# The causal mask of the second attention: a VectorE minimum instead of matmuls

## The chip, the cores and the metric

One core of one Trainium2 chip runs the whole program. The metric is the device time of one execution, in microseconds. The kernel before took 3099.48 us (median of 3 runs, 3081.88 to 3100.42).

## What is computed

Four stages over x of shape (4, 1024, 256), each with a residual sum and a layer norm: a gated linear attention, a mixture of experts, a differential attention, a second mixture of experts. The change lies in the third, whose core is:

```python
s1 = jnp.einsum('bhqd,bhkd->bhqk', q1, k1) * scale      # 16 heads, head dim 16, 1024 x 1024
s2 = jnp.einsum('bhqd,bhkd->bhqk', q2, k2) * scale
s1 = jnp.where(causal, neg, s1)
s2 = jnp.where(causal, neg, s2)
a1 = jax.nn.softmax(s1, axis=-1)
a2 = jax.nn.softmax(s2, axis=-1)
attn = a1 - lam[None, :, None, None] * a2
out = jnp.einsum('bhqk,bhkd->bhqd', attn, v)
```

There are 4 sequences x 16 heads x 2 maps = 128 causal maps of 1024 x 1024.

## The kernel before

`Layer1Attention` handles the maps four at a time. Four maps (two heads, two maps each) make one **pass**; there are 32 passes, four to a **unit** (half of one sequence's heads). Each map owns 32 of the 128 contraction rows of TensorE (head dim 16, one row more for a constant, the rest padding), so that the products of four maps can run at once in four row groups.

The softmax takes each row's maximum first. A pass therefore has two halves:

- `maxima` (L1303): for every query row, the maximum of the scores. Score products (L1323, tile `sc`, queries on partitions) fill one PSUM bank of 512 columns; VectorE reduces the bank's blocks of 128 keys to their maxima with the sign turned (L1330, into `top`). The lower triangle of 8 x 8 blocks is cut into nine banks (`banks`, L1293 to L1299): the first two hold the eight diagonal blocks, four each; the next four hold blocks 0 to 3 of one query row; the last three hold the rest. In blocks on the diagonal, keys after the query have to be kept out.
- `numerators` (L1358): the transposed scores (L1385, tile `sa`, keys on partitions), with the maximum subtracted by the extra contraction row, then the exponential on ScalarE (L1391) into `e`, and on GpSimd an affine select (L1401) that clears the part above the diagonal. `values_of` (L1427) multiplies `e` by the values into `oa`.

Between the halves, `least` (L1338) combines `top` on VectorE (L1344), transposes it on TensorE (L1348), copies it (L1350) and sends four rows into `qT` by DMAs on SP's queue (L1353). The second half of a pass runs 22 steps behind the first (`LAG`), so two passes overlap.

The order is written out by hand, in `steps`, and holds for TensorE, GpSimd, VectorE and ScalarE alike. A pass has `STEPS` = 20 steps. Step t takes bank t // 2 for maps 0 and 1 (t even) or maps 2 and 3 (t odd), for t up to 17, and beside it the numerators of an earlier pass for the other two maps. So each step has four streams of products: two `sc` and two `sa`, issued in turn, one product of each (zip_longest, and the `todo` loop). Each stream ends with its reduction or its exponential. A step with four blocks in its bank issues four products of 128 columns per map, one with a single row block issues one of 512. After every even step come the products of `values_of` for the item before; after any step at most one job: one that is due (the transposed output `tpo`, L1441; `least`; the output projection `yo` of an earlier sequence), or one that prepares the next unit (`inputs`, `turn` with `qkp`, `values` with `vp`, `to_slots` with `tps`). VectorE's and GpSimd's small work is put off and released by a budget per step (`put_off`, `catch_up`).

All `sc` and `sa` tiles share one pool of six PSUM banks (`pp`). A new tile takes the bank that was given back first in the order of the program. A step whose four streams have as many products each gives back in the order sc, sa, sc, sa; a step whose `sc` have more products than its `sa` gives back both `sa` first.

The mask before: in the diagonal banks, each map's first product is identity (bfloat16, 128 x 128) times a constant of 0 and -1e30 (L1316, 512 columns, all 128 rows), which opens the accumulation; the scores are then added to it. These two products per step (one for each map) are issued ahead of the step's other products, by the `next(halves[-1])` at the end of `maxima`. `set_up` makes the constants (L1119 to L1126), under the first expert layer. With nine banks in order, the diagonal ones are steps 0 to 3 of each pass: 4 steps x 2 products x 32 passes = 256.

Of the kernel before, what the change touches and what calls it, by code (L numbers as in the profile page):

```python
# [11 lines left out]

F32 = mybir.dt.float32
AF = mybir.ActivationFunctionType
ALU = mybir.AluOpType
# [3 lines left out]
P = 128  # L19
# [632 lines left out]
class Router:  # L652
# [58 lines left out]
    def work(self, plan, proj, norm):  # L711
# [89 lines left out]
        def choose(i, key):  # L801
# [7 lines left out]
            def begin():  # L809
                nonlocal steps  # L810
                steps = choice(c, sp, lg.t[:, 0:n, :], n, got)
                next(steps)

            j = add("DVE", 0.3, key, begin, [*cur["jc", i], done[0]], use=[lg])
            j = add("ACT", 0.3, key, lambda: next(steps), [j], table="exp")
            oh = [None]

            def pick():
                next(steps, None)
                oh[0] = sp.tile([P, n, E], F32, tag="oh", name="oh")  # L820
                nc.vector.tensor_tensor(oh[0], got[1], got[2], ALU.add)
# [229 lines left out]
class Layer1Attention:  # L1051
# [11 lines left out]
    QC = 512  # L1063
# [7 lines left out]
    def set_up(self, c, wqkT, bqk, wvT, bv, woT, bo, hnw, lqk, trig):  # L1071

        tc, nc, ident = c.tc, c.nc, c.ident
        UH, NS = self.UH, self.NS
        BIG = 3.0e38
        wp = self.wp

        wqk_s = wp.tile([P, DC, 2, 512], F32)
        nc.sync.dma_start(wqk_s, wqkT.rearrange("(c p) u f -> p c u f", p=P))
        wv_s = wp.tile([P, DC, D], F32)  # L1080
        nc.sync.dma_start(wv_s, wvT.rearrange("(c p) f -> p c f", p=P))
        wo_s = wp.tile([P, DC, D], F32)
# [12 lines left out]
        bo_b = wp.tile([P, D], F32)  # L1095
        nc.sync.dma_start(bo_b, bo.partition_broadcast(P))


        tr = wp.tile([P, NT, 2, 3, 8], F32)
        nc.sync.dma_start(tr, trig.rearrange("(t p) u k f -> p t u k f", p=P))  # L1100


        lam = wp.tile([P, AH, 2], F32)
        nc.vector.memset(lam, 1.0)
        ls = wp.tile([P, 2, AH], F32)
        with tc.tile_pool(name="a1_l", bufs=1, reuse_waits="tile") as lpool:
            lq = lpool.tile([P, 4, AH, HD], F32)
            nc.sync.dma_start(lq, lqk.partition_broadcast(P))
            lp = lpool.tile([P, 2, AH, HD], F32)
            nc.vector.tensor_tensor(lp[:, 0], lq[:, 0], lq[:, 1], ALU.mult)  # L1110
            nc.vector.tensor_tensor(lp[:, 1], lq[:, 2], lq[:, 3], ALU.mult)
            nc.vector.tensor_reduce(ls, lp, AX.X, ALU.add)
        nc.scalar.activation(ls, ls, AF.Exp)
        ld = wp.tile([P, AH], F32)
        nc.vector.tensor_tensor(ld, ls[:, 1, :], ls[:, 0, :], ALU.subtract)
        nc.vector.tensor_scalar(lam[:, :, 1], ld, LAMBDA_INIT, None, ALU.subtract)


        BF = mybir.dt.bfloat16  # L1119
        maskneg = wp.tile([P, 4, P], BF)  # L1120
        ident16 = wp.tile([P, P], BF)
        with tc.tile_pool(name="a1_k", bufs=1, reuse_waits="tile") as kp:
            mask32 = kp.tile([P, P], F32)
            make_causal_mask(nc, mask32, mask_val=-1e30)
            nc.vector.tensor_copy(maskneg, bc(mask32, 1, 4))
            nc.vector.tensor_copy(ident16, ident)  # L1126

        qks, vas, tops = [], [], []  # L1130
        for i in range(2):
            w = wp.tile([P, 2, NS, SL], F32, tag=f"qks{i}", name=f"qks{i}")
            nc.gpsimd.memset(w, 0.0)
            nc.gpsimd.memset(w[:, 1, :, HD : HD + 1], 1.0)
            qks.append(w)
        for i in range(2):
            va = wp.tile([P, NT, UH * VW + SL - VW], F32, tag=f"va{i}", name=f"va{i}")
            nc.gpsimd.memset(va, 1.0)
            vas.append(va)
            top = wp.tile([P, 4, NT, 8], F32, tag=f"top{i}", name=f"top{i}")  # L1140
            nc.gpsimd.memset(top, BIG)
            tops.append(top)
        self.wqk_s, self.wv_s, self.wo_s, self.bqk_b, self.bv_b, self.bo_b = wqk_s, wv_s, wo_s, bqk_b, bv_b, bo_b
        self.tr, self.lam, self.maskneg, self.ident16 = tr, lam, maskneg, ident16
        self.qks, self.vas, self.tops = qks, vas, tops

    def run(self, c, keep, B, combine):
# [20 lines left out]
    def steps(self, c, B, combine):  # L1168
        tc, nc, ident = c.tc, c.nc, c.ident
        UH, NG, NS, QC, NQ = self.UH, self.NG, self.NS, self.QC, self.NQ  # L1170
        pp, po, pm, bp, sp, ee, st = self.pp, self.po, self.pm, self.bp, self.sp, self.ee, self.st
        wqk_s, wv_s, wo_s, bqk_b, bv_b, bo_b = self.wqk_s, self.wv_s, self.wo_s, self.bqk_b, self.bv_b, self.bo_b
        tr, lam, maskneg, ident16 = self.tr, self.lam, self.maskneg, self.ident16
        xTs, o, kTs, qTs = {}, {}, {}, {}
        self.o = o

# [119 lines left out]
        banks = [([(i, i, i + 1) for i in range(4)], (slice(0, 4), slice(7, 8)), True)]  # L1296
# [6 lines left out]
        def maxima(n, t):  # L1303

            u, g = divmod(n, NG)
            kT, qT, top = kTs[u], qTs[u], self.tops[n % 2]
            k, pair = divmod(t, 2)
            parts, (ri, rk), diag = banks[k]
            halves = []
            for s in (2 * pair, 2 * pair + 1):  # L1310
                sl = slice(SL * s, SL * s + SL)

                def matmuls(s=s, sl=sl):
                    sc = pp.tile([P, QC], F32, tag="sc", name="sc")
                    if diag:
                        nc.tensor.matmul(  # L1316
                            sc, lhsT=ident16, rhs=maskneg.rearrange("p b k -> p (b k)"), start=True, stop=False,
                        )
                        yield
                    at = 0  # L1320
                    for m, (i, k0, k1) in enumerate(parts):
                        w = (k1 - k0) * P
                        nc.tensor.matmul(  # L1323
                            sc[:, at : at + w], lhsT=qT[sl, g, ts(i, P)], rhs=kT[sl, g, k0 * P : k1 * P],
                            start=not diag, stop=not diag or m == len(parts) - 1,
                        )
                        at += w
                        yield
                    out = top[:, s, ri, rk]
                    nc.vector.tensor_reduce(  # L1330
                        out, sc.rearrange("p (a b k) -> p a b k", a=out.shape[1], k=P), AX.X, ALU.max, negate=True,
                    )

                halves.append(matmuls())
                if diag:
                    next(halves[-1])
            return halves

        def least(n):
# [156 lines left out]
        for s in range(N * STEPS + LAG):  # L1496
            now = s
            catch_up(ROOM)
            n1, t1 = divmod(s, STEPS)
            n2, t2 = divmod(s - LAG, STEPS)  # L1500
            first = maxima(n1, t1) if n1 < N and t1 < STEPS - 2 else []
            second = numerators(n2, t2) if n2 >= 0 else []

# [13 lines left out]
            u, k = divmod(s, US)  # L1517
            if u + 1 < U and k == LAG + 2:
                prep = prepare(u + 1)
            if s % (2 * US) == LAG + 4 and s > 2 * US:  # L1520
                b = s // (2 * US) - 1
# [249 lines left out]
```

## Time and profile before

| | |
|---|---|
| median of 3 runs | 3099.48 us (3081.88 to 3100.42) |
| profiled execution, its own time | 3090.43 us |
| its span, first to last instruction | 3088.7 us |
| mean granted TensorE clock | 0.978 |
| stage of the second attention, from the first mask product to the last reduction | 1266.4 to 2762 us |
| 1152 reductions, L1330 | 738.8 us busy, 685 ns each |

The columns of the views used below. A busy row gives an engine's busy time, its share of the span, and the number of instructions. The chain of work that ended last is followed back from the last instruction; its shares tell which engine's and which line's work set the end. A row of a group or of the timeline has the line, engine, operation, output tile <- input tiles, partitions x elements and the count; in the groups the busy time and the mean of one in ns stand behind the bar, then the idle time of the engine before them with what ended it; in the timeline each row begins with start and length in us. A wait row reads: who waited, for whom, us in total, times, the longest. PE is TensorE's products and PEld its weight loads; the ends of products are modelled, since they are pipelined, so the distance from one start to the next tells more than a length.

### The profile page before, as it was taken

Reading aid. Unit: us, or ns where it says so; the run is one execution under the profiler, and the core shown is the slowest. Engines: PE = TensorE matmul, PEld = TensorE weight load, DVE = VectorE, ACT = ScalarE, POOL = GpSimd, SP = SyncE. Lnnn points to the kernel's source line nnn. Section 1 sums busy time; section 2 is a strip of 40 time slices with the busy share of each in tenths; the row PEclk is TensorE's granted clock in tenths of the full one; section 3 lists DMA queues with packets and bytes.
Section 4 is the critical chain, followed back from the end, with each engine's and each line's share of the span. In section 5 each row is a group of like instructions: output and inputs, shape, how many; then the busy total and the mean of one; then the engine's idle time right before and its main releaser. Section 6 shows DMA issues by size and latency. Waiting matters only on the chain.

```text
span 3088.7 us, 49688 instructions
## 1 busy us (share of the span) xinstructions
PE 2962.2 (96%) x19863; PEld 1803.9 (58%) x19880; DVE 1660.0 (54%) x3755; ACT 1127.7 (37%) x2175; POOL 1020.0 (33%) x1587
## 2 busy tenths in 40 slices
PE   9999999799999997899999999999999999999999
PEld 4656556588888886544554455454555555545544
DVE  4555566411111112776566775667666666652766
ACT  5444443111111111145554454544545455553000
POOL 1131333311111112174444644436444353231100
PEclk9999999899999998899999999999999999998999
DMA  9610101355554452000000000000000000001000
GB/s 336 206 42 14 42 18 65 126 188 184 187 176 174 179 187 100 5 25 5 2 1 7 18 7 2 1 3 22 7 2 2 2 1 2 2 2 57 18 18 19
DMA packets 83417, 189.32 MB, mean 61 GB/s; under 512 B 10145, under 2 KB 68274, under 8 KB 78194
## 3 DMA queue, kind: packets, MB, share of 16 engines
q0 software_dynamic: 15504, 119.03, 10.7%
q1 hardware_dynamic: 66322, 66.31, 6.7%
q8 instruction: 157, 2.57, 0.4%
q10 hardware_dynamic: 1360, 0.80, 0.1%
q14 instruction: 74, 0.61, 0.1%
HBM read 129.23 MB, written 56.36 MB: 60 GB/s over the span
## 4 chain that ended last, share of the span: by engine, by line
PE 85%; DVE 5%; POOL 4%; ACT 3%; issue 2%; DMA 1%; SPq 0%; POOLq 0%; DVEq 0%
PE sc L1323 16%; PE oa L1427 9%; PE sa L1385 9%; PE pj L141 9%; PE yp L141 7%; PE gpb L141 7%; PE upb L141 7%; PE ypb L141 7%; PE qkp L141 4%; PE tps L1227 2%; PE sc L1316 2%; POOL rows L854 2%; PE op L561 1%; DVE top L1330 1%; PE tpo L1441 1%
## 5 line engine op out<-in xcount | busy, mean ns | idle before, releaser
L1330 DVE TENSOR_REDUCE top<-sc 128x4 f32<-128x512 f32 x1152 | 738.8, 685 | 332.0 <-PE sa L1385 165.6
L1391 ACT ACTIVATE e<-sa 128x512 f32<-128x512 f32 (+1 forms) x1280 | 642.4, 553 | 716.8 <-PE sa L1385 487.6
L1385 PE MATMUL sa<-qT,kT 32*128 32x512 f32 (+3 forms) x3072 | 787.3, 526 | 0.7 <-DVE top L1330 0.4
L1323 PE MATMUL sc<-kT,qT 32*128 32x128 f32 (+2 forms) x5120 | 733.7, 384 | 4.2 <-DVE top L1330 4.2
L1323 PEld LDWEIGHTS sc<-kT,qT 32*128 32x128 f32 x5120 | 404.7, 189 | 279.7 <-DVE top L1330 125.5
L1401 POOL TENSOR_SCALAR_AFFINE_SELECT e<-e 128x256 f32<-128x256 f32 x512 | 202.0, 407 | 611.9 <-ACT e L1391 611.4
L1385 PEld LDWEIGHTS sa<-qT,kT 32*128 32x128 f32 x3072 | 310.3, 185 | 94.2 <-issue 35.2
L1020 DVE TENSOR_TENSOR hT<-upb,sgb 128x512 f32<-128x512 f32 x117 | 80.9, 692 | 504.5 <-PE upb L141 501.4
L1427 PE MATMUL oa<-e,va 128*32 128x512 f32 (+3 forms) x3072 | 318.7, 500 | 25.2 <-POOL e L1401 22.3
L141 PE MATMUL yp<-w,xT 128*128 128x512 f32 x512 | 229.8, 596 | 0.0
L141 PE MATMUL gpb<-nTb,w 128*128 128x256 f32 x936 | 222.9, 381 | 0.6 <-DVE nTb L1000 0.6
L141 PE MATMUL upb<-nTb,w 128*128 128x256 f32 x936 | 221.7, 380 | 0.0
L141 PE MATMUL ypb<-w,hT 128*128 128x256 f32 x936 | 208.5, 379 | 0.0
L141 PEld LDWEIGHTS gpb<-nTb,w 128*128 128x128 f32 x936 | 178.8, 191 | 25.5 <-DVE nTb L1000 1.0
L993 POOL DMA_INDIRECT xg<-rows,xi x78 | 73.7, 945 | 362.9 <-PE tx L997 350.0
L141 PEld LDWEIGHTS upb<-nTb,w 128*128 128x128 f32 x936 | 178.1, 190 | 24.3
L141 PEld LDWEIGHTS ypb<-w,hT 128*128 128x128 f32 x936 | 174.9, 190 | 22.2
L1019 ACT ACTIVATE sgb<-gpb 128x512 f32<-128x512 f32 x117 | 69.8, 597 | 282.5 <-PE gpb L141 282.5
L1427 PEld LDWEIGHTS oa<-e,va 128*32 128x32 f32 x3072 | 67.8, 109 | 178.3 <-issue 89.6
L141 PEld LDWEIGHTS yp<-w,xT 128*128 128x128 f32 x512 | 93.5, 190 | 98.6 <-issue 96.6
L1618 DVE SCALAR_TENSOR_TENSOR x<-yp,comb,x 128x256 f32<-128x256 f32 x256 | 121.9, 482 | 45.1 <-PE yp L141 38.7
L165 POOL TENSOR_TENSOR ln_r<-ln_v,neghalf 128x1 f32<-128x1 f32 x96 | 53.6, 559 | 252.3 <-DVE ln_v L162 252.0
(257 smaller groups left out, 3645.6 us busy)
## 6 DMA issues: line engine op xcount, KB each, us to landing
rows<-zeros SPq DMA_DIRECT2D x8, 4096.0 KB
f_outs<-yb SPq DMA_DIRECT2D x39, 256.0 KB
xTt<-in_xT SPq DMA_DIRECT2D x8, 512.0 KB
x<-in_x SPq DMA_DIRECT2D x32, 128.0 KB
out_x<-y SPq DMA_DIRECT2D x32, 128.0 KB
qT<-nmT SPq DMA_DIRECT2D x128, 4.0 KB
wi<-in_e_wiT SPq DMA_DIRECT2D x8, 256.0 KB
wo<-in_e_wo SPq DMA_DIRECT2D x8, 256.0 KB
```

Source lines behind the costliest of these rows:

```text
L141: nc.tensor.matmul(out, lhsT=l, rhs=r, start=i == 0, stop=i == len(pairs) - 1)
L854: s = nc.gpsimd.indirect_dma_start(self.rows, bass.IndirectOffsetOnAxis(ap=ri[0][:, k, t : t + 1], axis=0), xn[t].t, None)
L993: nc.gpsimd.indirect_dma_start(x, None, rows, bass.IndirectOffsetOnAxis(ap=xi[:, i, j : j + 1], axis=0))
L1019: nc.scalar.activation(sg, gps, AF.Silu)
L1020: nc.vector.tensor_tensor(hT[:, f : f + 2, :], ups, sg, ALU.mult)
L1323: nc.tensor.matmul(sc[:, at : at + w], lhsT=qT[sl, g, ts(i, P)], rhs=kT[sl, g, k0 * P : k1 * P], start=not diag, stop=not diag or m == len ...
L1330: nc.vector.tensor_reduce(out, sc.rearrange("p (a b k) -> p a b k", a=out.shape[1], k=P), AX.X, ALU.max, negate=True,)
L1385: nc.tensor.matmul(sc[:, at : at + QC - q0], lhsT=kT[sl, g, ts(j, P)], rhs=qT[sl, g, qc * QC + q0 : (qc + 1) * QC], start=True, stop=True,)
L1391: nc.scalar.activation(e[:, half, 0:w], sc[:, 0:w], AF.Exp)
L1401: nc.gpsimd.affine_select(out=e[:, :, at : at + P], in_=e[:, :, at : at + P], pattern=[[0, 2], [1, P]], compare_op=ALU.is_ge, fill=0.0, ba ...
L1427: nc.tensor.matmul(oa[SL * s : SL * s + SL, q0:QC], lhsT=va[:, j, h * VW : h * VW + SL], rhs=es_[n, k, s // 2][:, s % 2, at : at + QC - q0 ...
L1618: nc.vector.scalar_tensor_tensor(acc, yp[:, k, :], comb[:, t % NT, e : e + 1], acc, ALU.mult, ALU.add)
```

## The change

The mask products go, and with them both constants. `set_up` makes one constant `most` (128 x 128, float32): 3.0e38 on and below the diagonal, -1e30 above it. In a diagonal bank the score products now open their own accumulation; VectorE then takes the minimum of the bank and `most` (repeated four times) into an SBUF tile `sm`, and the reduction reads `sm` instead of the bank. The bank is given back by the minimum. The order of the nine banks differs between the map pairs: the two diagonal banks come at steps 2 and 10 for maps 0 and 1, at steps 7 and 15 for maps 2 and 3.

```diff
-        BF = mybir.dt.bfloat16
-        maskneg = wp.tile([P, 4, P], BF)
-        ident16 = wp.tile([P, P], BF)
-        with tc.tile_pool(name="a1_k", bufs=1, reuse_waits="tile") as kp:
-            mask32 = kp.tile([P, P], F32)
-            make_causal_mask(nc, mask32, mask_val=-1e30)
-            nc.vector.tensor_copy(maskneg, bc(mask32, 1, 4))
-            nc.vector.tensor_copy(ident16, ident)
+        most = wp.tile([P, P], F32)
+        nc.gpsimd.memset(most, BIG)
+        nc.gpsimd.affine_select(
+            out=most, in_=most, pattern=[[-1, P]], compare_op=ALU.is_ge, fill=-1e30, base=0, channel_multiplier=1,
+        )
...
-            parts, (ri, rk), diag = banks[k]
+            parts, (ri, rk), diag = banks[((2, 0, 3, 4, 5, 1, 6, 7, 8), (2, 3, 4, 0, 5, 6, 7, 1, 8))[pair][k]]
...
                     sc = pp.tile([P, QC], F32, tag="sc", name="sc")
-                    if diag:
-                        nc.tensor.matmul(
-                            sc, lhsT=ident16, rhs=maskneg.rearrange("p b k -> p (b k)"), start=True, stop=False,
-                        )
-                        yield
                     at = 0
-                    for m, (i, k0, k1) in enumerate(parts):
+                    for i, k0, k1 in parts:
                         w = (k1 - k0) * P
                         nc.tensor.matmul(
                             sc[:, at : at + w], lhsT=qT[sl, g, ts(i, P)], rhs=kT[sl, g, k0 * P : k1 * P],
-                            start=not diag, stop=not diag or m == len(parts) - 1,
+                            start=True, stop=True,
                         )
                         at += w
                         yield
+                    if diag:
+                        full, sc = sc, sp.tile([P, QC], F32, tag="sm", name="sm")
+                        nc.vector.tensor_tensor(
+                            sc.rearrange("p (b k) -> p b k", k=P), full.rearrange("p (b k) -> p b k", k=P),
+                            bc(most, 1, QC // P), ALU.min,
+                        )
                     out = top[:, s, ri, rk]
                     nc.vector.tensor_reduce(
                         out, sc.rearrange("p (a b k) -> p a b k", a=out.shape[1], k=P), AX.X, ALU.max, negate=True,
                     )

                 halves.append(matmuls())
-                if diag:
-                    next(halves[-1])
```

More of the change, by code (lines that the diff above doesn't have):

```diff
@@ L9 @@
 from concourse.bass import ts
-from concourse.masks import make_causal_mask, make_identity
+from concourse.masks import make_identity
 from concourse._compat import with_exitstack
@@ L1143, in set_up @@
         self.wqk_s, self.wv_s, self.wo_s, self.bqk_b, self.bv_b, self.bo_b = wqk_s, wv_s, wo_s, bqk_b, bv_b, bo_b
-        self.tr, self.lam, self.maskneg, self.ident16 = tr, lam, maskneg, ident16
+        self.tr, self.lam, self.most = tr, lam, most
         self.qks, self.vas, self.tops = qks, vas, tops
@@ L1172, in steps @@
         wqk_s, wv_s, wo_s, bqk_b, bv_b, bo_b = self.wqk_s, self.wv_s, self.wo_s, self.bqk_b, self.bv_b, self.bo_b
-        tr, lam, maskneg, ident16 = self.tr, self.lam, self.maskneg, self.ident16
+        tr, lam, most = self.tr, self.lam, self.most
         xTs, o, kTs, qTs = {}, {}, {}, {}
```

## The prediction

> **What bounds the kernel now.** I read the page first, for the place of the second attention in the span and in the chain of work that ended last; then the span cut into passes; then lines 1316, 1323 and 1330 and their waits; then single steps in the timeline.
>
> ```profile
> PE 2962.2 (96%) x19863; PEld 1803.9 (58%) x19880; DVE 1660.0 (54%) x3755; ACT 1127.7 (37%) x2175; POOL 1020.0 (33%) x1587
> ...
> PE sc L1323 16%; PE oa L1427 9%; PE sa L1385 9%; PE pj L141 9%; PE yp L141 7%; PE gpb L141 7%; PE upb L141 7%; PE ypb L141 7%; PE qkp L141 4%; PE tps L1227 2%; PE sc L1316 2%; POOL rows L854 2%; PE op L561 1%; DVE top L1330 1%; PE tpo L1441 1%
> ```
>
> On this page PE is the bound and the mask (L1316) is 2% of the chain, some 60 us. Three passes of the 32 (one pass is four attention maps, 20 steps), by the view of stretches; columns: stretch, length, busy time of PE, PEld, DVE, ACT, POOL, then clock and DMA:
>
> ```profile
> 1266.70:1292.50 25.80, 23.83 (x172) 16.91 (x171) 22.60 (x38) 1.59 (x2) 0.00 (x0) 0.74 0.00 1
> 1919.50:1972.50 53.00, 52.95 (x441) 27.19 (x442) 31.71 (x59) 26.84 (x55) 26.92 (x41) 1.00 0.01 2
> 2639.20:2681.10 41.90, 41.15 (x377) 20.71 (x377) 27.67 (x53) 21.39 (x45) 13.19 (x26) 1.00 0.01 2
> ```
>
> The first is pass 0, which has no numerators beside it. The second is pass 14, which also prepares the next unit (qkp, tps, vp). The third is pass 29, which prepares nothing. By the starts of L1323, 16 passes are like 29 (40.6 to 45.5 us), 14 like 14 (50 to 58 us), pass 31 has nothing behind it.
>
> PE reads busy nearly throughout, but the digits hide stalls inside a step. Two adjacent steps of pass 29:
>
> ```profile
> 2662.58 0.69 PE L1323 MATMUL sc<-kT,qT 32*128 32x512 f32 x1
> ...
> 2664.49 0.69 PE L1385 MATMUL sa<-qT,kT 32*128 32x512 f32 x1
> ...
> 2665.54 1.05 PE L1427 MATMUL oa<-e,va 128*32 128x512 f32 x5
> ```
> ```profile
> 2663.74 1.29 DVE L1330 TENSOR_REDUCE top<-sc 128x4 f32<-128x512 f32 x2 [0.24 <-PE sa L1385]
> ```
>
> A step that waits for nothing takes 1.07 us (1938.46 to the next group at 1939.53). These two take 2.96 instead of 2.14: the second half of the second step starts at 2664.49, just after the first reduction (2663.74 + 0.69 = 2664.43) and the first exponential have emptied a bank. Six banks serve four streams, so a step's last two banks are those the step before has to empty first. Over the stage:
>
> ```profile
> PEld sc L1323 <- DVE top L1330: 125.5, 185, 2.0
> ```
>
> And the price of the mask itself, in pass 14 (start, length):
>
> ```profile
> 1922.55 0.59 PE L1316 MATMUL sc<-maskneg,ident 128*128 128x512 bf16 x2
> 1923.07 0.37 PE L1323 MATMUL sc<-kT,qT 32*128 32x128 f32 x1
> ```
>
> Start to start, two mask products hold PE for 0.52 us; there are 128 such pairs, 67 us in all.
>
> Skill, first place. Pass 29 shows 41.15 of 41.90 us of PE and only 20.71 of PEld. The Trainium skill ("Trainium Kernel Development and Optimization", Performance Expectations) calls matmul busy time a bad measure, because matmuls are pipelined, and weight-load time a good one. Going by PE busy, the whole 67 us would come back; by the page, only passes like 14 are full and would return 14 x 4 x 0.52 = 29 us.
>
> **Part 1, mask products removed.** At most 128 x 0.52 = 67 us; at least nothing, where PE waits for a bank at the same place anyway.
>
> **Part 2, minimum added.** 256 of 128x512 f32, PSUM and SBUF in. Not in the trace; same operands and size as L1235:
>
> ```profile
> L1235 DVE TENSOR_TENSOR qk<-qkp,bqk_b 128x512 f32<-128x512 f32 x56 | 38.7, 691 | 70.9 <-PE qkp L141 70.9
> L1330 DVE TENSOR_REDUCE top<-sc 128x4 f32<-128x512 f32 x1152 | 738.8, 685 | 332.0 <-PE sa L1385 165.6 <-PE sc L1323 164.7 <-PE oa L1427 0.4
> ```
>
> I take 0.69. Bounds: 0.42 (L1449, 256 elements) and 0.80 (L1045, 256 elements, two inputs and a scalar). The reduction then reads SBUF: L1461 takes 0.275 for 128 elements and L1344 0.417 for 256, in line 0.70 for 512; I keep 0.69. Independent operations overlap (two reductions take 1.29), dependent ones don't: 0.03 from the end of L1443 to the start of L1445. A diagonal step's DVE block is therefore min 0.69, reduce to 1.41, min to 2.04, reduce to 2.74, counted from 0.03 after the products: 1.45 us more than the 1.29 of now, 186 us over 128 steps. Its two banks are free at 0.72 and 2.04.
>
> **Part 3, diagonal banks moved** from steps 0 to 3 of a pass to steps 2, 7, 10, 15. Queued behind the block on DVE are the next step's reductions: the first ends 3.4 us after the diagonal step's products (2.68 + 0.69), where now it ends 1.8 after them if the steps follow at once (1.07 + 0.03 + 0.69). PE issues in order, so a bank that comes late holds all four streams. The step after a diagonal one takes banks that ACT empties; the second one after it is the one that meets the late reduction.
>
> Walk through pass 29, from its start at 2639.20, with the durations above:
> - Steps 1 and 2. Now step 2 begins at 5.20, behind the products at 2.08 (yo), two mask pairs and step 1. Without masks it could begin at 4.02. But step 1's reductions are behind the DVE work of yo (L1558 to L162, 3.31 to 4.61) and the first ends at 5.3, so step 2 ends at 6.5 (now 6.37). Both masks between were cover for this wait.
> - Step 4 begins at 9.3 (now 9.20): of three mask pairs, 1.56 us, nothing is left.
> - Step 7 (diagonal) and 8: step 8 needs ACT's banks; ends at 19.0 (now 18.92). Step 9 needs the first reduction of step 8, at 20.6 behind the block: ends 21.7 instead of 20.56, 1.1 late.
> - Steps 10 and 15: the steps just behind them have two or four score parts and so hand on ACT's banks first; the steps two behind wait for ACT as now. The lag settles at 0.85.
> - End: +0.85, less the mask pair that opens the next pass, 0.52: **+0.33**.
>
> Same walk in pass 14: a job of 0.5 to 1.9 us stands behind most steps, so banks are free earlier than needed. Step 2 still waits for the yo chain (ends 6.5, now 6.87), step 4 ends 0.4 early, steps 7 to 12 keep and widen that to 0.7, since job and output separate step 9 from the block: -0.6 to -0.7, and -0.5 for the opening pair: **-1.1**.
>
> Pass 0 goes by DVE already, as its chain shows:
>
> ```profile
> 1271.65 1.14 PE sc L1323 x16
> 1272.79 18.02 DVE top L1330 x30
> ```
>
> Now 24.4 us to its last reduction (1266.39 to 1290.81). After: one step 1.09, 36 reductions at 0.60, 8 mins at 0.725: 28.5. **+4.1**, less one opening pair: +3.6.
>
> Sum: 14 x -1.1 = -15.4; 16 x 0.33 = +5.3; pass 0 +3.6; pass 31 +0.85: **-5.7 us**.
>
> **Edits with one answer.** Setup loses a cast (L1125, 0.42 us at 588.7) and a copy on DVE, keeps a memset and a select on POOL (0.23, 0.30); it lies under the first expert layer's products (PE 9 in those slices). Uncovered: under 1 us. No DMA is added or moved; SP still sends four rows per pass (L1353, 0.73 apart). But step 2 moves 1.2 us towards them: the last lands about 1.85 after its issue (2767.09 to 2768.9 in the tail), 4.5 after the pass starts, and the numerators of step 2 need it. Where yo stands in step 0 they wait longer for the reduction; in passes 1 to 9, without yo, this landing takes that place. POOL gets no step of its own; its selects follow ACT.
>
> **Rivals.**
> *Full gain.* PE is the bound and stalls merely move: -67 and pass 0's +4 give -63, 3030; half of it kept gives 3062. For it: 85% of the chain is PE. Against: 2662.58 to 2665.54 above.
> *DVE sets the pace (slower).* One mechanism: the reduction two steps behind a diagonal step, late at step 9 by 1.1 us, is late behind all four. Then each pass loses 4 x (1.1 - 0.52) = 2.3 us, 31 x 2.3 + 4 = +75; 3168. It decides from 1.3 us lost per diagonal step (+31 in all), 2.5 times the 0.5 that the walk gives; min and SBUF reduction each 0.15 longer would do it, since the block then reaches step 9 in passes like 14 too. For it: 125.5 us of waits now, DVE busy from 27.7 to 33.5 of 41.9. Against: steps 12 and 17 take banks from ACT.
> *No work saved.* If the score products were to start no earlier anywhere, only DVE's excess in pass 0 would show: +4, 3097, within the forecast's class.
>
> Skill, second place. PE waits 125.5 us for L1330 to empty banks. The Trainium skill ("TensorEngine Tiling (Array Packing)", PSUM Bottleneck) says that row tiling speeds up the products but not the emptying of PSUM, which can become the bottleneck; it speaks against this change. By the rule one would forecast the second rival, 3168; by the walk, the sum above.
>
> **How the numbers follow.** The profiled execution took 3090.43 us (span 3088.7, 1.7 around it); the median of three is 3099.48, their lowest 3081.88. The mean of these four is 3093; less 5.7: 3087. Chances: walk right within some 0.7 us per pass, 3066 to 3112, 0.55; full gain (3030 to 3066) 0.20; DVE pace (3112 to 3168) 0.25. For 8 in 10 I leave out the far half of each rival: 3045 to 3132. About 1% (31 us) is what a measurement can tell. Faster by more: the full gain and little else, 0.22; slower: most of the DVE case, 0.23; within: 0.55.
>
> **What would show it.** Right: PE busy falls by some 50 us without the span following; DVE rises by about 180; waits of L1323 for DVE rise from 125.5 to over 170; pass 0 about 29, pass 29 about 42, pass 14 about 52. Step 9 late in pass 29 and not in 14. Wrong: pass 29 at 40 (full gain) or 44 (DVE), mins far from 0.69, a wait for the landing of qT rows that outlasts the reduction.

## The result, and the profile after

The changed kernel takes 3121.3 us (median of 14 runs, 3107.33 to 3132.66), the kernel before 3096.9 us beside it (14 runs, 3081.88 to 3104.01). The ratio is 1.0086, 95% interval 1.0071 to 1.0101: slower by 24 us, where 6 us less was forecast. The profiled span is 3115.2 us against 3088.7, at a granted clock of 0.977 against 0.978.

The page of the kernel after, engines and chain:

```profile
PE 2959.6 (95%) x19624; PEld 1799.9 (58%) x19624; DVE 1818.6 (58%) x4009; ACT 1134.7 (36%) x2175; POOL 1018.4 (33%) x1587
...
PE sc L1317 11%; PE sa L1383 10%; PE pj L141 9%; PE oa L1425 8%; PE yp L141 7%; PE gpb L141 7%; PE upb L141 6%; PE ypb L141 6%; DVE top L1330 4%; PE qkp L141 4%; DVE sm L1325 2%; PE tps L1225 2%; ACT e L1389 2%; PE op L561 1%; POOL rows L854 1%
```

(Line numbers shift: the score products are now L1317, the minimum L1325, the reduction still L1330, the transposed scores L1383, their exponential L1389.) The mask is gone from the chain, and VectorE has taken its place and more: L1330 went from 1% to 4%, and the minimum has 2%. PE lost the 256 mask products, yet its busy time fell by only 2.6 us. The same three passes as before, in the view of stretches (length, busy PE, PEld, DVE, ACT, POOL, clock, DMA):

```profile
1265.67:1295.04 29.37, 25.76 (x162) 19.69 (x162) 27.52 (x45) 2.03 (x3) 0.00 (x0) 0.60 0.00 1
1933.87:1986.02 52.14, 51.53 (x432) 26.10 (x432) 36.01 (x67) 26.81 (x54) 26.43 (x40) 1.00 0.01 2
2666.79:2710.62 43.83, 41.94 (x368) 20.79 (x368) 32.88 (x61) 21.77 (x44) 13.13 (x26) 1.00 0.01 2
```

Pass 0 and pass 14 came as forecast (29 and 52); pass 29 did not: 43.83 us, where 42 was forecast and 44 had been named as the sign of VectorE setting the pace. It has nine PE records fewer than before and is 1.93 us longer.

The new instructions cost what was assumed (busy us and mean ns behind the bar, then the idle time of VectorE before them):

```profile
L1325 DVE TENSOR_TENSOR sm<-sc,most 128x512 f32<-128x512 f32 x256 | 175.4, 685 | 92.9 <-PE sc L1317 73.7 <-PE sa L1383 19.2
L1330 DVE TENSOR_REDUCE top<-sm 128x4 f32<-128x512 f32 x256 | 176.2, 688 | 8.8
L1330 DVE TENSOR_REDUCE top<-sc 128x4 f32<-128x512 f32 x896 | 569.7, 683 | 120.6 <-PE sa L1383 63.2 <-PE sc L1317 55.9
```

The minimum takes 0.685 us (forecast 0.69), and reading SBUF instead of PSUM saves the reduction nothing (688 against 683 ns). What changed is who waits. Waits of the weight loads for VectorE, over the stage:

```profile
PEld sc L1317 <- DVE top L1330: 92.9, 150, 3.3
...
PEld sa L1383 <- DVE top L1330: 65.3, 105, 1.4
...
PEld sc L1317 <- DVE sm L1325: 27.4, 45, 1.7
...
PEld sa L1383 <- DVE sm L1325: 6.4, 21, 1.0
```

They sum to 192 us. Before they were 136.7: the 125.5 us shown there, and 11.2 for the transposed scores. A reader who follows L1317 alone sees 120.3 us and calls it an improvement; the added waits stand in front of `sa`, the other user of the same six banks.

Where the 26.5 us of span came in, from the starts of each pass's first score product in both traces, after less before:

| | forecast | measured |
|---|---|---|
| 14 passes like pass 14 | -15.4 | -1.9 |
| 14 passes like pass 29 | +4.6 | +19.9 |
| passes 11 and 19 | +0.7 | +10.9 |
| pass 0 | +3.6 | +3.6 |
| pass 31 | +0.85 | +2.4 |
| ahead of the stage's first score product | 0 | -1.0 |
| after the stage's last score step begins | 0 | -7.3 |

The last row most likely belongs to the one execution of before: its granted clock was 0.84 in the 57 us around the last numerators, against 0.94 in the kernel after. Eleven other kernels below have 319.5 to 326.4 us there, and one 328.7; before had 329.3.

### The profile page after: what moved, and what is told of

The parts are those of the page before. It is cut to its first block, busy times and chain, and to the rows that moved or that the text cites. A ratio compares the mean times of both kernels' runs of the same rounds, so it can differ in the third digit from the quotient of the medians.

```text
span 3115.2 us, 49419 instructions
## 1 busy us (share of the span) xinstructions
PE 2959.6 (95%) x19624; PEld 1799.9 (58%) x19624; DVE 1818.6 (58%) x4009; ACT 1134.7 (36%) x2175; POOL 1018.4 (33%) x1587
## 4 chain that ended last, share of the span: by engine, by line
PE 80%; DVE 10%; ACT 3%; POOL 3%; issue 2%; DMA 1%; SPq 0%; POOLq 0%; DVEq 0%; another core or an unknown queue 0%
PE sc L1317 11%; PE sa L1383 10%; PE pj L141 9%; PE oa L1425 8%; PE yp L141 7%; PE gpb L141 7%; PE upb L141 6%; PE ypb L141 6%; DVE top L1330 4%; PE qkp L141 4%; DVE sm L1325 2%; PE tps L1225 2%; ACT e L1389 2%; PE op L561 1%; POOL rows L854 1%
## 5 line engine op out<-in xcount | busy, mean ns | idle before, releaser
L1389 ACT ACTIVATE e<-sa 128x512 f32<-128x512 f32 (+1 forms) x1280 | 646.5, 553 | 738.2 <-PE sa L1383 458.5
L1383 PE MATMUL sa<-qT,kT 32*128 32x512 f32 (+3 forms) x3072 | 830.6, 524 | 14.7 <-DVE top L1330 11.2
L1317 PE MATMUL sc<-kT,qT 32*128 32x128 f32 (+2 forms) x5120 | 732.3, 388 | 10.9 <-DVE top L1330 7.7
L1330 DVE TENSOR_REDUCE top<-sc 128x4 f32<-128x512 f32 x896 | 569.7, 683 | 120.6 <-PE sa L1383 63.2
L1317 PEld LDWEIGHTS sc<-kT,qT 32*128 32x128 f32 x5120 | 399.4, 189 | 236.2 <-DVE top L1330 92.9
L1383 PEld LDWEIGHTS sa<-qT,kT 32*128 32x128 f32 x3072 | 318.1, 184 | 151.6 <-DVE top L1330 65.3
L1325 DVE TENSOR_TENSOR sm<-sc,most 128x512 f32<-128x512 f32 x256 | 175.4, 685 | 92.9 <-PE sc L1317 73.7
L1330 DVE TENSOR_REDUCE top<-sm 128x4 f32<-128x512 f32 x256 | 176.2, 688 | 8.8
```

The lines of the kernel that those rows point to most:

```text
L1317: nc.tensor.matmul(sc[:, at : at + w], lhsT=qT[sl, g, ts(i, P)], rhs=kT[sl, g, k0 * P : k1 * P], start=True, stop=True,)
L1325: nc.vector.tensor_tensor(sc.rearrange("p (b k) -> p b k", k=P), full.rearrange("p (b k) -> p b k", k=P), bc(most, 1, QC // P), ALU.min,)
L1330: nc.vector.tensor_reduce(out, sc.rearrange("p (a b k) -> p a b k", a=out.shape[1], k=P), AX.X, ALU.max, negate=True,)
L1383: nc.tensor.matmul(sc[:, at : at + QC - q0], lhsT=kT[sl, g, ts(j, P)], rhs=qT[sl, g, qc * QC + q0 : (qc + 1) * QC], start=True, stop=True,)
L1389: nc.scalar.activation(e[:, half, 0:w], sc[:, 0:w], AF.Exp)
```

## The experiments

Each ratio is to the kernel before, run on the same chip between its runs, with its 95% interval.

### What is the removal worth, and what the order?

First, neither mask nor minimum. Here the maxima of the diagonal blocks take in keys after the query as well; the exponentials there are still cleared by GpSimd, and a quotient of exponentials doesn't depend on the number subtracted. `neither_new` is the kernel after with its order of banks, `neither_old` the same with the order of before.

```diff
# against the kernel after: neither_new
-                    if diag:
-                        full, sc = sc, sp.tile([P, QC], F32, tag="sm", name="sm")
-                        nc.vector.tensor_tensor(
...
# and for neither_old also
-            parts, (ri, rk), diag = banks[((2, 0, 3, 4, 5, 1, 6, 7, 8), (2, 3, 4, 0, 5, 6, 7, 1, 8))[pair][k]]
+            parts, (ri, rk), diag = banks[k]
```

> The old order of the banks, with neither mask products nor minimum: the maxima of the diagonal blocks then take in later keys too, which the select after the exponential still clears. Three theories for the 24 us lost. Queue (the mask's time does come back, and VectorE's block of minimum and reduction costs more than that through banks given back late): 3050 to 3065 us, passes like 29 about 1 us shorter than before, passes like 14 about 1.6 us. Cover (the mask products only filled waits for banks, their removal pays nothing): 3090 to 3100. Order (the new places of the diagonal banks are what costs): the full gain, 3030 to 3045.

> The kernel after without the minimum: new order, no mask of the maxima at all. Queue: 3050 to 3070, within 10 us of the same with the old order. Cover: 3090 to 3100. Order: 25 us or more above the same with the old order.

Measured: `neither_old` 3058.78 us, 0.9884 (0.9857 to 0.9911); `neither_new` 3041.39 us, 0.9841 (0.9818 to 0.9864). The first is in the range of the queue reading, the second 9 us below it; both are far under the range of the cover reading. Against before, the passes of `neither_old` like 29 are 1.1 us shorter in the mean, as expected, those like 14 only 0.4, where 1.6 was expected.

Then the two crossings: `mask_new` is the kernel before with only the new order, `min_old` the kernel after with the old order.

> The kernel before with nothing but the new order of the banks, mask by matmuls. Queue: 3085 to 3105, as before within 10 us. Cover: the same, or up to 10 above, as the masks no longer stand where the waits are. Order: 3115 to 3130.

> The kernel after with the old order: four blocks of minimum and reduction in four steps running, 11 us of VectorE in some 8.5 us of steps. Queue: slower than after, 3130 to 3180. Cover: as after, 3115 to 3130. Order: well under before, 3045 to 3070.

Measured: `mask_new` 3086.59 us, 0.9984 (0.997 to 0.9998); `min_old` 3211.97 us, 1.0382 (1.036 to 1.0404). The first is where the queue reading put it and some 30 us under the range of the order reading; the second is beyond every range, 32 us above that of the queue.

Last, both at once: the new order, with the mask products kept and the minimum added (one `sm` buffer instead of the pool's own number, and `most` made as the stage begins).

> New order, mask by matmuls and the minimum on top of it (it changes nothing then; one buffer for its output instead of two, the constant made at the start of the stage). If the costs of the two add up, the same 77 us as without the masks lie on the 3087 of the new order with masks: 3155 to 3170. If the mask products cover the block's waits, less: 3120 to 3140.

Measured: 3180.29 us, 1.0289 (1.0261 to 1.0317), 10 us above the range expected if the costs add up. Start to start over passes 1 to 30, against `neither_new`, the two together cost 119.0 us, the masks alone 39.8 and the minimum alone 69.6: neither covers the other.

What follows. Taking the mask products away pays, whatever the order: 32 us with the old order (before to `neither_old`), 45 with the new one (`mask_new` to `neither_new`), 63 with the minimum present (2.0% between `mask_min` and the kernel after), of the 67 us that their starts bounded; by the intervals each of the three is uncertain by some 10 us. So the removal was not hidden, and the new order is no cost: it gives 4 us with masks and 17 without. The minimum costs 2.45% of the time of before with the new order (`neither_new` to after), 76 us, and 5.0% with the old one, 154 us. The change is a gain of 45 and 4 us, and a loss of 76.

The page of `neither_new` has the same number of PE instructions as the kernel after:

```profile
PE 2899.8 (96%) x19624; PEld 1786.3 (59%) x19624; DVE 1647.6 (54%) x3753; ACT 1129.8 (37%) x2175; POOL 1020.1 (34%) x1587
```

With equal products, PE busy differs by 60 us and PEld by 14. So busy time of products isn't a count of their work. The Trainium skill ("Trainium Kernel Development and Optimization", Performance Expectations) calls it a bad measure, because matmuls are pipelined, and these two pages agree that it is one. What the prediction drew from it, that only full passes would return the mask (29 us), failed: 32 to 63 us came back. Nor did the rows shown support it: weight loads take 51% of pass 14 and 49% of pass 29 (27.19 of 53.00 and 20.71 of 41.90 us), so this measure doesn't set the two apart.

### Where does the minimum cost?

Start to start of every step (by its first score product; the last two steps of a pass have none and count with step 17), summed over passes 1 to 30, a kernel with the added work less the same order without it, in us. The diagonal banks of the new order are steps 2, 7, 10 and 15; the kernels in the table that are not yet told follow below.

| less its "neither" | pass 0 | step 2 | 3 | 4 | 5 | 9 | 10 | 11 | 12 | others | passes 1-30 |
|---|---|---|---|---|---|---|---|---|---|---|---|
| after | 5.8 | 3.1 | 2.4 | **42.3** | 0.1 | **27.7** | -3.7 | 0.4 | -0.1 | -2.6 | 69.6 |
| min_first | 4.7 | -1.0 | 1.7 | 28.9 | 1.0 | 22.4 | -3.7 | -0.1 | 0.1 | 0.8 | 50.1 |
| min_defer | 4.7 | -1.2 | 3.7 | 12.8 | 17.2 | 0.7 | 9.0 | -0.2 | 0.3 | 6.6 | 48.9 |
| norm_late | 5.8 | -2.4 | 0.2 | 36.1 | 2.8 | 27.7 | -3.7 | 1.9 | -0.8 | -1.2 | 60.6 |
| act_pool | 0.8 | 1.0 | 14.0 | 2.7 | 13.7 | -0.2 | 1.2 | 5.7 | 1.2 | 17.2 | 56.5 |
| min_placed | 5.8 | 2.4 | 7.8 | 2.0 | 0.0 | 7.8 | 3.7 | 14.9 | 13.9 | -0.6 | 51.9 |
| first_placed | 4.7 | 1.4 | 5.7 | 2.9 | 0.0 | 4.2 | 4.3 | 7.5 | 10.5 | -4.6 | 31.9 |

In the kernel after, nearly the whole cost in these passes lies in two steps of the twenty: step 4, two behind the first diagonal step, and step 9, two behind the second. Steps 12 and 17, two behind the others, lose nothing. In pass 29 step 4 loses 1.64 us and step 9 loses 1.43, and no other step loses anything that lasts. Step 4 of pass 29, in the timeline of the kernel after (start, length):

```profile
2673.74 0.69 DVE L1325 TENSOR_TENSOR sm<-sc,most 128x512 f32<-128x512 f32 x1 [0.73 <-PE sa L1383]
...
2675.78 0.69 DVE L1330 TENSOR_REDUCE top<-sm 128x4 f32<-128x512 f32 x1
2675.92 0.18 PEld L1317 LDWEIGHTS sc<-kT,qT 32*128 32x128 f32 x1 [0.17 <-DVE sm L1325]
...
2676.39 0.61 DVE L167 TENSOR_SCALAR x<-xb,ln_mv,ln_r 128x256 f32<-128x256 f32 x1
...
2676.92 1.27 DVE L1330 TENSOR_REDUCE top<-sc 128x4 f32<-128x512 f32 x2
2677.65 0.94 PEld L1383 LDWEIGHTS sa<-qT,kT 32*128 32x128 f32 x6 [1.41 <-DVE top L1330]
```

The same place in pass 29 of `neither_new` (reductions are L1324 there, transposed scores L1377):

```profile
2602.02 1.29 DVE L1324 TENSOR_REDUCE top<-sc 128x4 f32<-128x512 f32 x2 [0.73 <-PE sa L1377]
...
2603.22 0.40 DVE L167 TENSOR_SCALAR x<-xb,ln_mv,ln_r 128x256 f32<-128x256 f32 x1
2603.54 1.28 DVE L1324 TENSOR_REDUCE top<-sc 128x4 f32<-128x512 f32 x2
2604.20 0.18 PEld L1377 LDWEIGHTS sa<-qT,kT 32*128 32x128 f32 x1
2604.28 0.18 PEld L1377 LDWEIGHTS sa<-qT,kT 32*128 32x128 f32 x1
```

Both kernels begin step 4 at 9.13 us of the pass (2675.92 less 2666.79, and 2604.20 less 2595.07). Four streams share the step, two of L1317 and two of the transposed scores. Without the minimum, the loads of the second transposed stream follow from 2604.28 without a stop: step 3's first reduction, begun at 2603.54, has emptied its bank 0.69 later, at 2604.23. With it, that reduction stands behind the block of four instead of two reductions, and behind L167, a layer norm's last step for an earlier sequence. It begins at 2676.92, is through at 2677.6, and six loads of the transposed scores begin at 2677.65, 1.73 us after the step did. No cover was left here: the bank came just in time before, and what VectorE gets more is lost at once.

Step 9, behind the block of step 7, is the wait that the prediction had named:

```profile
2687.08 0.69 DVE L1330 TENSOR_REDUCE top<-sm 128x4 f32<-128x512 f32 x1
...
2687.68 2.47 DVE L1330 TENSOR_REDUCE top<-sc 128x4 f32<-128x512 f32 x4
2688.26 0.60 ACT L1389 ACTIVATE e<-sa 128x512 f32<-128x512 f32 x1 [0.62 <-PE sc L1317]
2688.42 0.29 PEld L1383 LDWEIGHTS sa<-qT,kT 32*128 32x128 f32 x2 [1.02 <-DVE top L1330]
```

Step 8's first reduction begins at 2687.68, behind the block; it is through at 2688.37, and the loads that waited 1.02 us begin at 2688.42. In `neither_new` the four reductions of steps 7 and 8 follow one another, and step 9's loads of the transposed scores begin 0.07 us after its first ones, which begin at 2613.55:

```profile
2611.67 2.49 DVE L1324 TENSOR_REDUCE top<-sc 128x4 f32<-128x512 f32 x4 [1.57 <-PE sc L1317]
...
2613.62 0.18 PEld L1377 LDWEIGHTS sa<-qT,kT 32*128 32x128 f32 x1
```

### The block's own order, and another engine

`min_first` issues both minima of a diagonal step, then both reductions; `min_defer` issues the reductions a step later, behind the next step's own. Both work on the kernel after.

```diff
+                    def reduce():
                         nc.vector.tensor_reduce(
...
+                    held.append(reduce) if diag else reduce()
...
# min_defer; min_first runs what is held right behind this step's own loop instead
+            late = held[:]
+            held.clear()
             while todo:
                 todo = [h for h in todo if next(h, self) is not self]
+            for reduce in late:
+                reduce()
```

> The kernel after, the two reductions of a diagonal step issued one step later, behind that step's own reductions; the minimum stays where it is. VectorE does the same work. Three readings of the 77 us that the minimum and its reduction cost between the kernel without them (3041) and after (about 3117 on that chip). Queue (the next step's reductions stand behind a block of 2.74 us): the block ahead of them shrinks to 1.3, most of the loss goes, 3045 to 3070. Throughput (VectorE has too little idle time in all): no change, 3110 to 3120. Own banks (the diagonal step's banks, given back by the minimum at 0.72 and 2.04 us, come too late): the second one comes at 1.3, 3085 to 3105.

> The kernel after with the order in the block changed: both minima first, then both reductions, in the same step. Queue: the block is shorter by what two dependent pairs cost, some 0.2 us, 3100 to 3115. Throughput: 3105 to 3117. Own banks: the second bank comes 0.7 us sooner, 3080 to 3100.

Measured: `min_defer` 3096.3 us, 1.0019 (1.0006 to 1.0033); `min_first` 3097.32 us, 1.0022 (1.0008 to 1.0036). The reading of the queue alone expected 3045 to 3070 of the first, and missed: it brought 21 us of the 76. That of throughput expected no change and missed too. That of the diagonal step's own banks had 3085 to 3105 and 3080 to 3100, and both times came in there; yet the traces speak against it. In `min_first` the two minima empty the diagonal banks as early as the reductions do in `neither_new` (within 0.01 us in pass 29 at steps 2, 7 and 15, and 0.12 us earlier at step 10; over all 30 passes 0.02 us earlier in the mean), and still 50.1 of the 69.6 us are lost. Step 4 of its pass 29 (the reduction is L1332 there, the transposed scores L1388; the pass starts at 2644.97):

```profile
2651.92 1.29 DVE L1325 TENSOR_TENSOR sm<-sc,most 128x512 f32<-128x512 f32 x2 [0.72 <-PE sa L1388]
...
2654.31 0.40 DVE L167 TENSOR_SCALAR x<-xb,ln_mv,ln_r 128x256 f32<-128x256 f32 x1
...
2654.63 1.28 DVE L1332 TENSOR_REDUCE top<-sc 128x4 f32<-128x512 f32 x2
2655.36 0.94 PEld L1388 LDWEIGHTS sa<-qT,kT 32*128 32x128 f32 x6 [0.95 <-DVE top L1332]
```

What decides is when the next step's first reduction begins. In pass 29, by how many us these events come later in the pass than in `neither_new` (`norm_late`, told below, puts off the layer norm of L167):

| | after | min_first | norm_late | min_defer |
|---|---|---|---|---|
| first reduction of step 3 begins | 1.65 | 1.18 | 0.98 | 0.00 |
| step 5 begins | 1.64 | 1.17 | 0.97 | 0.00 |
| first reduction of step 8 begins | 3.08 | 2.37 | 2.42 | 1.19 |
| step 10 begins | 3.07 | 2.36 | 2.41 | 1.19 |

In 24 of the 30 passes of the kernel after, too, step 4 loses what that reduction is late, within 0.05 us; passes 1, 11 and 19 lose 1.3 to 2.3 us more. `min_first` makes the block 0.25 us shorter (2.48 us against 2.73 in pass 29), and L167 behind it took 0.40 us instead of 0.61 (the last section says more on its length); together that is the 0.47 us by which the reduction comes sooner. `min_defer` leaves step 3's reductions as early as without the minimum, and step 4 of pass 29 loses nothing; but the reductions put off then stand before step 4's own, and step 5 loses 1.11 us. So deferring empties step 9 of its loss (0.7) but moves a part one step on, to step 10 (9.0), and splits step 4's between 4 and 5.

`act_pool` takes the emptying off VectorE: ScalarE copies the diagonal bank to SBUF, GpSimd writes -1e30 above the diagonal, VectorE reduces a step later as in `min_defer`.

```diff
-                        nc.vector.tensor_tensor(
...
+                        nc.scalar.copy(sc, full)
+                        nc.gpsimd.affine_select(
+                            out=sc.rearrange("p (b k) -> p b k", k=P), in_=sc.rearrange("p (b k) -> p b k", k=P),
+                            pattern=[[0, QC // P], [-1, P]], compare_op=ALU.is_ge, fill=-1e30,
```

> The kernel after with the mask put on by other engines: ScalarE copies the diagonal bank to SBUF, GpSimd's affine select writes -1e30 above the diagonal, and VectorE reduces the copy one step later. VectorE's time is that of the kernel without a mask. Queue and throughput: 3045 to 3070. If instead any added emptying of a bank costs as much, because ScalarE's two copies of 0.6 us now hold the exponentials and their banks: 3090 to 3120.

Measured: 3095.43 us, 1.0006 (0.9985 to 1.0027). The groups of its page:

```profile
L1326 POOL TENSOR_SCALAR_AFFINE_SELECT sm<-sm 128x512 f32<-128x512 f32 x256 | 156.5, 635 | 208.5 <-ACT sm L1325 206.9
L1325 ACT COPY sm<-sc 128x512 f32<-128x512 f32 x256 | 138.4, 603 | 14.7 <-PE sc L1317 14.7
```

VectorE is as busy as in `neither_new` (1650.5 us busy against 1647.6) and ScalarE is 40% busy, and still the kernel loses 1.7% to `neither_new`. The time is in the range of the reading that any added emptying costs as much, but its reason, the exponentials behind the copies, isn't what pass 29 shows in steps 3 and 5, to which the loss has moved. Step 3 loses 0.41 us there to another copy on ScalarE: `ot` (L1441), which stands behind the two new ones, begins 8.21 us into the pass instead of 7.44, and the transposes `tpo` wait for it 1.16 us instead of 0.76. Step 5 loses 0.76 us to VectorE: step 4's first reduction begins at 11.62 us instead of 10.50, behind the two reductions put off, and step 5's loads wait for it. So VectorE's queue still decides in step 5, with no more work in it than without a mask; ScalarE's copies with the reductions left in place were not tried. The Trainium skill ("TensorEngine Tiling (Array Packing)", PSUM Bottleneck) says that after row tiling the emptying of PSUM may become the limit, and advises to use both ScalarE and VectorE for it. The first half fits the waits of this case; the second, tried here with the reductions put off, gained no more than putting them off alone (1.0006 and 1.0019, with overlapping intervals).

### The place, and what else VectorE does there

`min_placed` puts the diagonal banks at steps 6, 9, 12 and 15, where step 4 is clear of them; `first_placed` has the minima first as well; `neither_placed` is the same order without the minimum.

```diff
-            parts, (ri, rk), diag = banks[((2, 0, 3, 4, 5, 1, 6, 7, 8), (2, 3, 4, 0, 5, 6, 7, 1, 8))[pair][k]]
+            parts, (ri, rk), diag = banks[((2, 3, 4, 0, 5, 6, 1, 7, 8), (2, 3, 4, 6, 0, 5, 7, 1, 8))[pair][k]]
```

> The kernel after with nothing but other places for the banks: diagonal ones at steps 6, 9, 12 and 15, each followed by a step whose score banks take two or four products. In the traces so far the block costs pass 29 1.64 us at step 4 and 1.43 at step 9, and nothing behind steps 10 and 15, whose next steps are of that kind and hand on ScalarE's banks first. If the place decides which bank is late, a plain pass loses under 0.5 us to the block and the kernel takes 3045 to 3070. If VectorE's added time counts wherever it stands: 3105 to 3125, as after.

> The same places, with both minima ahead of both reductions as in the run before that showed 3097 with the places of after. Place theory: 3040 to 3065, at most 8 us better than the other order within the block. Throughput: 3085 to 3105.

> The same places with neither minimum nor mask products in the maxima (later keys count in the diagonal blocks' maxima): what the places alone do. Both theories: 3030 to 3055; the distance of the two runs above from this one is the price of the block.

Measured: `min_placed` 3118.75 us, 1.0102 (1.007 to 1.0134); `first_placed` 3085.6, 0.9989 (0.9973 to 1.0005); `neither_placed` 3048.54, 0.9876 (0.9843 to 0.9909). The reading by place expected 3045 to 3070 of the first, and fails: step 4's loss does go (42.3 to 2.0), but 29 us turn up in steps 11 and 12, and the placement alone gives nothing. In pass 29 it is the same queue again: step 10's first reduction, behind the block of step 9, begins at 24.08 us of the pass instead of 22.25 in `neither_placed`, and step 11 loses 0.66 us; step 11's first reduction then ends at 26.35, and the loads of step 12 that need its bank begin at 26.40. With the minima first it is worth 30 us against after (1.0086 to 0.9989), the best kernel that keeps a minimum, and no slower than before; the reading by place had expected 3040 to 3065 of it. The ranges of throughput held for both kernels. But `min_placed`, `first_placed`, `min_first`, `min_defer` and `norm_late` (below) run the same 4009 VectorE instructions at ratios from 0.9989 to 1.0102, so their sum doesn't decide.

`norm_late` tests L167 by itself: the layer norm behind `yo` is put off by ten steps in the kernel after.

```diff
-                put_off(parts, [0.0, 0.5, 0.0])
+                put_off(parts, [0.0, 0.5, 0.0], 10)
```

> The kernel after, with the layer norm behind the output projection put off by ten steps instead of one. If the reductions of steps 1 and 3 are late because this layer norm's VectorE work (L1556 to L167) stands before them, step 4 of pass 29 loses about 0.7 us to the block instead of 1.64, and step 2 begins sooner: 3085 to 3105. If the layer norm is beside the point: 3112 to 3122.

Measured: 3096.39 us, 1.0024 (1.0011 to 1.0037), as expected, 19 us less than after by the ratios; in the two profiled executions, 15.6 us apart, the stage is 9.6 us shorter. Step 4 in pass 29:

```profile
2664.62 1.28 DVE L1330 TENSOR_REDUCE top<-sc 128x4 f32<-128x512 f32 x2
2665.36 0.94 PEld L1383 LDWEIGHTS sa<-qT,kT 32*128 32x128 f32 x6 [0.89 <-DVE top L1330]
```

The late loads begin 10.19 us into the pass (pass start 2655.17) instead of 10.86: the 0.67 us are about L167's 0.61. Step 5 still begins 0.97 us later than in `neither_new` (0.7 was expected), so the block alone makes step 4 late.

Passes 11 and 19 show the same with more in the queue. They hold the sum and layer norm of the first expert layer (L1045, L158 to L167). In pass 11 of the kernel after, the score products of step 2 end at 8.74 us of the pass, 1795.66; its first minimum starts at 1799.35:

```profile
1797.22 1.47 DVE L167 TENSOR_SCALAR x<-x,ln_mv,ln_r 128x256 f32<-128x256 f32 x1
...
1799.35 0.68 DVE L1325 TENSOR_TENSOR sm<-sc,most 128x512 f32<-128x512 f32 x1
```

Between the two stand only such instructions, and those of the layer norm behind `yo`. This pass is 5.5 us longer than before, of which the minimum is 4.2 (against `neither_new`).

**The fastest.** `neither_new`, 3041.39 us, is 1.6% faster than before and 2.4% faster than after: here the maxima need no mask at all. (By the arithmetic of the quotient, that holds while no excluded score lies so far above its row's others that their exponentials vanish.)

**What stays open.** Of the 76 us, 30 were recovered by order and place together; alone, deferring gave 21, the minima first 20, the layer norm put off 19, and the place none. That the late next reductions are the cost, and not the later emptying of the diagonal banks, is shown by `min_first` and by the table of pass 29. What passes 1, 11 and 19 lose beyond that at step 4, and why step 12 of `min_placed` loses 0.65 us in some passes like 29 and up to 2.21 in others, wasn't found.

## Why the prediction was wrong

The forecast was 3087 us and no change beyond 1%; the time is 3121.3, within the range, and slower by 0.86%, so within the 1% that the likeliest class allowed. But the sign was given as a gain of 6 us, and the loss of 24 us is measured; 3121 lies in the band that was given to VectorE setting the pace, at a chance of 0.25. By its steps:

- **The price of the minimum: right.** 0.685 us against 0.69; the SBUF reduction 0.688 against 0.69. DVE busy rose by 159 us (forecast about 180), and the block of step 2 in pass 29 took 2.73 us (forecast 2.74).
- **Part 1, the mask at most 67 us: right, and nearer to its upper bound** than the walk had it. The walk called both mask pairs between steps 0 and 2 cover for a wait and counted little more than the opening pair. By starts, before against `neither_old`, the pairs of steps 0 and 2 come back (12.9 and 15.3 us over the passes), those of steps 1 and 3 do not (1.1 and -0.5), and step 3 is 6.6 us longer without the masks. In the new order, `neither_new` against `mask_new`, more comes back, 39.8 us in these passes against 19.2; there no two diagonal steps follow one another.
- **The step that failed: "Step 4 begins at 9.3 (now 9.20): of three mask pairs, 1.56 us, nothing is left."** Step 4 does begin there, at 9.13. But a step has four streams, and the walk let the step's end follow its start. Its own rule, "the second one after it is the one that meets the late reduction", was applied to step 9, behind step 7, and not to step 4, behind step 2. There the last stream waits until 10.86 us into the pass, for a reduction behind the block and L167: 1.64 us that the walk put at nothing. The term "16 x 0.33" was mis-sized by this: passes like 29 lose 1.4 us each in the mean (19.9 over 14), 1.9 in pass 29.
- **Step 9, "1.1 late": right** in place and nearly in size, 1.43 against `neither_new`, 1.5 against before.
- **"Steps 10, 15: the steps just behind them ... hand on ACT's banks first": right.** Steps 12 and 17 lose -0.1 and -0.2 us in all 30 passes. As a rule for other places the reason doesn't hold: step 10 of `min_placed` has two score parts as well, and step 11 loses 0.66 us in pass 29.
- **"Same walk in pass 14 ... -1.1": right for pass 14 (-0.86), wrong as a price for 14 passes.** They gave -1.9 in place of -15.4. Pass 14 loses 0.85 us in step 4; passes 13, 17, 21 and 25 lose 1.64 there, and pass 1 loses 3.76. The jobs of a preparing pass differ, and one walk stood for all.
- **Passes 11 and 19** were counted as like pass 29. Their spans in the profile before, 45.4 us against 41.9, were known ("40.6 to 45.5") and said that something else runs in them; it runs on VectorE. 10.9 us in place of 0.7.
- **Pass 0: right**, +3.6.
- **No wait for the landing of the `qT` rows** took the place of the reduction's: the waits of L1383 for it are 1.9 us in the whole stage, three times, and as much in `neither_new`.

Of the rivals, "DVE sets the pace" had the right resource. Its condition, late behind all four diagonal steps, did not come about: two of four are late, by 1.64 and 1.43 us in pass 29 where it had taken 1.1, and its 3168 us lies above the result. Its threshold is a slip: by its own sum, 31 x 4 x (t - 0.52) + 4, a loss of 31 us comes from t = 0.74 us per diagonal step, not from 1.3; measured are 0.58 in the mean (69.6 over 30 passes and 4 steps). "Full gain" is what the change without its minimum would have brought nearly: `neither_new` at 3041 against 3030 to 3062. "No work saved" fell with the removal's 32 to 63 us. Of the signs announced, "PE busy falls by some 50 us" did not appear (2.6); it would have been `neither_new`'s (62.4). The sign "waits of L1323 for DVE rise from 125.5 to over 170" failed as well (120.3 on that line; the rise stands in front of the transposed scores), and the 44 us named for pass 29 came. Step 9 is late in pass 29 and not in 14, as announced.

## What to carry to other kernels

When two engines' products share a few PSUM banks, price a new vector instruction at every step that takes a bank the engine gives back afterwards, at each stream inside the step and not only at its start, and list all else that stands in that engine's queue there. Here, where the waiting loads already began within 0.1 us of the release, the price was the whole delay of that release (the table of pass 29). And before a mask is made cheaper, ask whether the quantity needs it: a maximum that is only subtracted doesn't.

## What the runs showed of the hardware beyond that

The same pass in the same kernel repeats to 0.01 us: passes 16, 20, 24, 28, 29 and 30 of `neither_new` and after differ by 2.89 to 2.90 us, so one step can be read from one pass there. Not in every kernel: in `min_placed` the same six passes take 42.60 to 44.22 us. A reduction of 128x512 from SBUF took as long as one from PSUM (688 and 683 ns). VectorE's L1045 and L167, 256 elements each, took up to 1.75 and 1.48 us in the kernel after, where L167 took 0.40 elsewhere. A GpSimd instruction runs beside each long one: over all 14 kernels the last step of the first expert layer's and this layer's norms is recorded 896 times; the 381 with nothing on GpSimd at that time took 0.39 to 0.42 us, and all 198 above 0.45 us had something there. Beside the 1.47 us above, for instance:

```profile
1797.27 1.28 POOL L1245 TENSOR_TENSOR qks<-qk,rot 128x512 f32<-128x512 f32 x1
```

That GpSimd lengthens them is likely by this, though no run tested it. The reductions from PSUM show nothing of the kind: 682 ns with at least 0.3 us of GpSimd work beside them, 683 without any.
